# A gated attention and mixture-of-experts block on one core: unwanted products between stages, attention begun with two batches, scaled queries, small first loads

## The chip, the cores and the metric

The program runs on one core of one Trainium2 chip. A core has five engines that run side by side and wait for each other through semaphores: TensorE (PE in the profile, PEld for its loading of stationary operands), VectorE (DVE), ScalarE (ACT), GpSimd (POOL) and SyncE (SP). Transfers between the chip's main memory and the on-chip memories are issued from queues of SP, ACT or POOL and run on 16 DMA engines. TensorE writes its products to PSUM, eight banks of 128 by 512 floats here. TensorE's clock is granted by the chip: the profile gives it as a share of full speed.

The metric is the device time of one execution in microseconds (us); lower is better.

## The reference

Two layers on x of shape (64, 128, 128), all float32. The first is cross-attention to a context of 77 rows per batch; the second a block in which each token picks few of 16 experts for its query, key, value and output projections, with self-attention inside a batch.

```python
def _L0_xattn_ref(batch, latent, Wk, Wq, Wv):
    keys = einsum('bpe,fe->bpf', batch, Wk)
    queries = einsum('ble,fe->blf', latent, Wq)
    values = einsum('bpe,fe->bpf', batch, Wv)
    weights = softmax(einsum('ble,bpe->blp', queries, keys) * scale, axis=-1)
    return einsum('blp,bpe->ble', weights, values)
...
    logits = xn @ sn - sigmoid(gates)
    gated = relu(logits)
    ...
    w = softmax(where(mask > 0, gated, -inf), axis=-1)      # few of 16 experts per token
    def moe_proj(p):
        y = einsum('nc,ech->neh', x, p)
        return einsum('ne,neh->nh', w, y)
    q, k, v = (moe_proj(p).reshape(b, t, -1) for p in (q_proj, k_proj, v_proj))
    scores = einsum('bth,bsh->bts', q, k) / sqrt(h)
    attn = softmax(scores, axis=-1)
    o = einsum('bts,bsh->bth', attn, v).reshape(n, h)
    out = einsum('enh,ehc->nc', einsum('ne,nh->enh', w, o), o_proj)
...
x = x + tanh(g_xattn[0]) * _L0_xattn_ref(ctx_1024, _layernorm(x), Wk, Wq, Wv)
x = x + tanh(g_ffn[0]) * _L0_ffn_ref(_layernorm(x), sim_matrix, gates, q_proj, k_proj, v_proj, o_proj)
```

## The kernel before

There are 8192 tokens, 64 tiles of 128. The kernel goes through five stages, one after the other.

`first_stage` (L193 on) does the cross-attention of all batches, four batches to a group, and picks each token's experts. It writes the new x and the expert weights to main memory as `xrow`, in batch order.

`order` (L678 on) sorts tokens by their pair of experts. It makes `place_i` (where each token goes) and `source` (which token stands at each sorted place). `source` comes from 64 accumulated products into the PSUM tile `pi` (L801); after the last one DVE reads `pi` (L811). A count, `flag`, is then read by all engines, and a branch chooses the sparse program (L1304) that this input takes.

`project` (L971 on) gathers the sorted rows with 64 indirect transfers issued by POOL (L980), makes the list of (tile, expert) items with 24 small products (`list_items`, L859) and then, for each item, a product of 128 by 128 by 384 (L1019) that DVE scales and adds up in `acc` (L1024, L1028). Each finished tile is scattered back to batch order in `qkvrow` by an indirect transfer of POOL (L997). The order of items is written out in `in_turn`.

`attend` (L1050 on) is the self-attention. SP loads q, k and v of a group of batches from `qkvrow` (L1068) once all scatters have landed; the groups have 1, 1, 2, 4, 4, ... batches. Each group is a stream of four steps: transposes of q and k with their copies to on-chip memory (`transposed`, L169 and L175; ACT copies q, DVE copies k); score products (L1087) and softmax (L148 row maximum, L150 its scaling by 1/sqrt(C), L155 exponentials); transposed exponentials; products with v (L1110), scaling by DVE into `o` (L1118) and one indirect scatter by POOL per batch to `orow`, sorted again (L1125). `in_steps` (L181) starts one more group at each step and advances all running ones by a step. Five output tiles `o` can be in flight.

`output` (L1137 on) loads the sorted attention rows four tiles at a time with SP (L1147, `fetch`), after all scatters of `attend`. PE transposes each tile (L1150), ACT copies the result (L1151), and for each item PE multiplies by the expert's output weights (L1176), and DVE adds the scaled product to x (L1180). Finished tiles are scattered by POOL to the result (L1158). Four tiles `og` of four token tiles each can be in flight.

A scheduler sets the order of instructions on each engine from the order of the calls and the data; each engine then runs its instructions strictly in that order. `LATER` is a dependency that only orders two instructions of one engine, `SYNC` one with a semaphore.

Of the kernel before, what the change touches and what calls it, by code (L numbers as in the profile page):

```python
# [10 lines left out]
F32 = mybir.dt.float32  # L11
# [11 lines left out]
def gated_xattn_moe_kernel(  # L23
# [33 lines left out]
    nc = tc.nc  # L57

    B, T, C = x.shape
# [82 lines left out]
    std = const.tile([P, B], F32, tag="std", name="std")  # L142
    flag = const.tile([1, 1], I32, tag="flag", name="flag")

    def softmax(small, psc, ex, n, scale=None, many=G):

        nm = small.tile([P, G], F32, tag="nm", name=f"nm_{n}")[:, :many]
        nc.vector.tensor_reduce(nm, psc, AX.X, ALU.max, negate=True)  # L148
        if scale is None:
            nc.vector.tensor_scalar_mul(nm, nm, SCALE)  # L150
        else:
            nc.vector.tensor_mul(nm, nm, scale)
        sums = small.tile([P, G], F32, tag="sums", name=f"sums_{n}")[:, :many]
        for j in range(many):
            nc.scalar.activation(  # L155
                ex[:, j, :],
                psc[:, j, :],
                AF.Exp,
                bias=nm[:, j : j + 1],
                scale=SCALE if scale is None else scale[:, j : j + 1],  # L160
                accum_out=sums[:, j : j + 1],
            )
        return sums

    def transposed(bank, pool, src, rows, cols, tag, n, copy=None, many=G):

        pt = bank(f"pt_{tag}_{n}")
        for j in range(many):
            nc.tensor.transpose(  # L169
                pt[:cols, j * rows : (j + 1) * rows],  # L170
                src[:, j, :],
                ident[:rows, :rows],
            )
        dst = pool.tile([cols, G * rows], F32, tag=tag, name=f"{tag}_{n}")
        (copy or nc.scalar.copy)(dst[:, : many * rows], pt[:cols, : many * rows])  # L175
        return dst

    def by_batch(rows, b0, n, lo, hi):
        return rows[b0 * T : (b0 + n) * T, lo:hi].rearrange("(b t) c -> t b c", t=T)

    def in_steps(streams, lag=1):  # L181

        running, step = [], 0
        while streams or running:
            if streams and step % lag == 0:
                running.append(streams.pop(0))
            for s in list(running):
                if next(s, "done") == "done":
                    running.remove(s)
            step += 1  # L190
# [487 lines left out]
    def order(ctx, begun, place_i, source, ahead):  # L678
# [106 lines left out]
        for b0 in range(0, B, K):  # L785
            r = slice(b0, b0 + K)
            nc.vector.tensor_tensor(
                at_hi[:, r, :],
                colh[:, None, :].to_broadcast([P, K, NTILE]),
                hi[:, r, None].to_broadcast([P, K, NTILE]),  # L790
                ALU.is_equal,
            )
            nc.vector.tensor_tensor(
                at_lo[:, r, :],
                col[:, None, :].to_broadcast([P, K, P]),
                lo[:, r, None].to_broadcast([P, K, P]),
                ALU.is_equal,
            )
            for b in range(b0, b0 + K):
                nc.scalar.mul(at_id[:, b, :], at_hi[:, b, :], ids[:, b : b + 1])  # L800
                nc.tensor.matmul(  # L801
                    pi[:, b // NB, :],
                    at_lo[:, b, :],
                    at_id[:, b, :],
                    start=(b % NB == 0),
                    stop=(b % NB == NB - 1),
                )

        R = [P, B // NB, NTILE]
        whose, found = t("whose", R), t("found", [P, NTILE])  # L810
        nc.vector.scalar_tensor_tensor(  # L811
# [159 lines left out]
    def project(ctx, source, items, given, xg, acc):  # L971
# [44 lines left out]

        def weighted(name, slot, w, s, there, add):
            py = ps.tile([P, 512], F32, tag="tmp", name=name)
            nc.tensor.matmul(  # L1019
                py[:, : 3 * C], slot, w_flat[:, bass.ds(w, 3 * C)], start=True, stop=True  # L1020
            )
            scale = xg[:, bass.ds(s, 1)]
            if add:
                nc.vector.scalar_tensor_tensor(  # L1024
                    there, py[:, : 3 * C], scale, there, ALU.mult, ALU.add
                )
            else:
                nc.vector.tensor_scalar(there, py[:, : 3 * C], scale, None, ALU.mult)  # L1028
# [11 lines left out]
        def more(i):  # L1040
# [2 lines left out]
            there = acc[:, bass.ds(at_acc.tile_of(i), 3 * C)]  # L1043
            weighted(f"pm_{i}", slot, at_w[2].of(i), at_s[2].tile_of(i), there, True)

        in_turn(ready, fixed, more, store, True, 3)
        return made

    @with_exitstack
    def attend(ctx, place_i, stored, acc):  # L1050

        io = ctx.enter_context(tc.tile_pool(name="io_c", bufs=5))
        work = ctx.enter_context(tc.tile_pool(name="work_c", bufs=3))
# [11 lines left out]
        def load(g):  # L1065
            b0, n = starts[g], sizes[g]
            qkv = acc[:, b0 * 3 * C : (b0 + n) * 3 * C].rearrange("p (b c) -> p b c", b=n)
            behind(nc.sync.dma_start(qkv, by_batch(qkvrow, b0, n, 0, 3 * C)), stored)  # L1068
            return qkv

        loaded = {g: load(g) for g in range(5)}
        made = []

        def group(g):
            b0, n = starts[g], sizes[g]
            qkv = loaded.pop(g)
            if g + 5 < len(sizes):
                loaded[g + 5] = load(g + 5)
            qT = transposed(bank, work, qkv[:, :, 0:C], P, C, "qT", g, many=n)
            kT = transposed(  # L1080
                bank, work, qkv[:, :, C : 2 * C], P, C, "kT", g, copy=nc.vector.tensor_copy, many=n
            )
            yield

            psc = bank(f"psc2_{g}").rearrange("p (b s) -> p b s", s=P)[:, :n, :]
            for j in range(n):
                nc.tensor.matmul(  # L1087
                    psc[:, j, :],
                    qT[:, j * P : (j + 1) * P],
                    kT[:, j * P : (j + 1) * P],  # L1090
                    start=True,
                    stop=True,
                )
            ex = work.tile([P, G, T], F32, tag="ex2", name=f"ex2_{g}")[:, :n, :]
            sums = softmax(small, psc, ex, f"f_{g}", many=n)
            yield

            gsum = small.tile([P, G], F32, tag="gsum2", name=f"gsum2_{g}")[:, :n]  # L1100
            nc.vector.reciprocal(gsum, sums)
            nc.vector.scalar_tensor_tensor(
                gsum, gsum, tg_f, std[:, b0 : b0 + n], ALU.mult, ALU.mult
            )
            exT = transposed(bank, work, ex, P, P, "ex2T", g, many=n)
            yield

            po = bank(f"po_{g}").rearrange("p (b c) -> p b c", c=C)[:, :n, :]
            for j in range(n):
                nc.tensor.matmul(  # L1110
                    po[:, j, :],
                    exT[:, j * P : (j + 1) * P],
                    qkv[:, j, 2 * C : 3 * C],
                    start=True,
                    stop=True,
                )
            o = io.tile([P, G, C], F32, tag="o", name=f"o_{g}")
            nc.vector.tensor_tensor(  # L1118
                o[:, :n, :], po, gsum[:, :, None].to_broadcast([P, n, C]), ALU.mult
            )  # L1120
            for j in range(n):
                b = b0 + j
                apart(
                    made,
                    nc.gpsimd.indirect_dma_start(  # L1125
                        orow,
                        bass.IndirectOffsetOnAxis(ap=place_i[:, b : b + 1], axis=0),
                        o[:, j, :],
                        None,
                    ),  # L1130
                )

        in_steps([group(g) for g in range(len(sizes))])
        return made

    @with_exitstack
    def output(ctx, source, items, xg, scattered, acc):  # L1137

        io = ctx.enter_context(tc.tile_pool(name="io_d", bufs=4))
        slots = ctx.enter_context(tc.tile_pool(name="slots_d", bufs=8))  # L1140
        ps = ctx.enter_context(tc.tile_pool(name="ps_d", bufs=8, space=bass.MemoryType.PSUM))
        oT = acc[:, : NTILE * P]
        rows_out = out.rearrange("b t c -> (b t) c")

        def fetch(t):
            og = io.tile([P, G, C], F32, tag="og", name=f"og_{t}")
            behind(nc.sync.dma_start(og, by_batch(orow, t, G, 0, C)), scattered)  # L1147
            pt = ps.tile([P, 512], F32, tag="tmp", name=f"pto_{t}")
            for j in range(G):
                nc.tensor.transpose(pt[:, j * P : (j + 1) * P], og[:, j, :], ident)  # L1150
            nc.scalar.copy(oT[:, t * P : (t + G) * P], pt)  # L1151

        made = []

# [13 lines left out]
        at_w = [Offsets(nc.tensor, items, 3, first) for first in (0, NTILE, NFIX)]  # L1168
        at_s = [Offsets(nc.vector, items, 4, first, SROW, C, E) for first in (0, NTILE, NFIX)]
        def ready(t):  # L1170
            if t % G == 0:
                fetch(t)

        def weighted(name, slot, w, s, there):
# [129 lines left out]
    with tc.If(most_active < 3) as sparse:  # L1304
        with tc.tile_pool(name="ordered", bufs=1) as ordered:
# [1 line left out]
            _, _, _, limits, facts, _, items_b = begun["pairs"]  # L1307
            given = (ahead, begun["met"], limits, facts, items_b)
            stored = project(source, items, given, xg, acc)
            scattered = attend(place_i, stored, acc)  # L1310
            output(source, items, xg, scattered, acc)
    with sparse.Else():
        dense()
# [42 lines left out]
```

## Time and profile before

| | |
|---|---|
| median of 3 runs | 642.78 us (641.19 to 646.51) |
| the profiled execution | 644.02 us, of which 642.3 are the span from first to last instruction |
| busy: PE / PEld | 457.9 / 337.7 us (71% / 53%) |
| busy: DVE / ACT / POOL | 371.1 / 232.9 / 298.2 us (58% / 36% / 46%) |
| granted clock of PE, mean | 0.846 |
| instructions | 9774 |

The costliest groups stand like this on the page: line, engine, operation, what is written from what, count, busy time, mean of one in ns, then the engine's idle time just before them and what ended most of it.

```profile
L1019 PE MATMUL py<-w_all,xT 128*128 x256 | 106.6, 512 | 31.0 <-issue 23.2
L1024 DVE SCALAR_TENSOR_TENSOR acc<-pm,xg,acc 128x384 f32 x104 | 63.8, 613 | 24.5 <-PE py L1019 12.9
L1125 POOL DMA_INDIRECT orow<-o,place_i x64 | 61.9, 967 | 52.6 <-DVE o L1118 16.8
L1158 POOL DMA_INDIRECT out_dram<-xg,source x64 | 62.0, 968 | 60.7 <-DVE xg L1180 50.3
L1180 DVE SCALAR_TENSOR_TENSOR xg<-pz,xg 128x128 f32<-128x128 f32 x128 | 41.9, 345 | 28.1 <-PE pz L1176 20.3
```

A float32 product is two records of PE (so 64 x 2 items of `pz` are 256 records), a transpose is one. "issue" is idle time for which the profile shows no reason, "remote" and "another core or an unknown queue" one whose releaser it can't name.

### The profile page before, as it was taken

To read this page: it belongs to the slowest core of one execution; us is meant where nothing else is said; L and a number is where in the kernel's file an instruction comes from. 1 tells how busy PE (TensorE), PEld (TensorE's weight loads), DVE (VectorE), ACT (ScalarE), POOL (GpSimd) and SP (SyncE) were. 2 spreads that over 40 slices of the span, in tenths; PEclk is the share of its full clock that TensorE was granted. 3 is DMA by queue.
4 is the path that set the end of the run, shared out by engine and by line. 5 is a ranking of instruction groups with operands and counts; after the bars stand their busy time and mean duration, and the time that the engine had idled before them with its cause. 6 is when DMAs were issued, how large, how long until landed. Compare 5 with 4: busy or idle time off the path is not lost. (4 is left out here: it accounts for less than half of the span.)

```text
span 642.3 us, 9774 instructions
## 1 busy us (share of the span) xinstructions
PE 457.9 (71%) x2467; PEld 337.7 (53%) x2467; DVE 371.1 (58%) x1196; ACT 232.9 (36%) x846; POOL 298.2 (46%) x328
## 2 busy tenths in 40 slices
PE   2999999756723226999999994677665457876771
PEld 1898986432411003555555552567555356765761
DVE  4379999977310014888888884244333225666552
ACT  2689898547000002232223120244433225332300
POOL 4134344400777760333422556165666604555564
PEclk9999999855855566999999998597978659899777
DMA  8954221210222220122211323895111143121111
GB/s 212 248 154 118 73 76 39 74 38 1 61 60 57 57 60 12 62 88 75 87 62 38 123 107 134 295 379 199 45 42 45 42 122 108 62 90 41 39 47 36
DMA packets 53173, 59.56 MB, mean 93 GB/s; under 512 B 6455, under 2 KB 44919, under 8 KB 53111
## 3 DMA queue, kind: packets, MB, share of 16 engines
q1 hardware_dynamic: 40928, 32.41, 16.7%
q0 software_dynamic: 10240, 25.71, 12.4%
q10 hardware_dynamic: 1943, 0.74, 0.6%
q8 instruction: 24, 0.39, 0.3%
q14 instruction: 38, 0.31, 0.2%
HBM read 33.14 MB, written 25.69 MB: 92 GB/s over the span
## 5 line engine op out<-in xcount | busy, mean ns | idle before, releaser
L1019 PE MATMUL py<-w_all,xT 128*128 x256 | 106.6, 512 | 31.0 <-issue 23.2
L997 POOL DMA_INDIRECT qkvrow<-acc,source x64 | 62.1, 970 | 99.4 <-DVE acc L1024 91.5
L1158 POOL DMA_INDIRECT out_dram<-xg,source x64 | 62.0, 968 | 60.7 <-DVE xg L1180 50.3
L1019 PE MATMUL pm<-w_all,slot 128*128 x208 | 86.9, 504 | 0.0
L1125 POOL DMA_INDIRECT orow<-o,place_i x64 | 61.9, 967 | 52.6 <-DVE o L1118 16.8
L980 POOL DMA_INDIRECT xg<-xrow,source x64 | 60.7, 948 | 44.8 <-issue 44.8
L1024 DVE SCALAR_TENSOR_TENSOR acc<-pm,xg,acc 128x384 f32 x104 | 63.8, 613 | 24.5 <-PE py L1019 12.9
L1019 PEld LDWEIGHTS py<-w_all,xT 128*128 128x128 f32 x256 | 45.5, 198 | 60.5 <-issue 32.5
L1028 DVE TENSOR_SCALAR acc<-py,xg 128x384 f32<-128x384 f32 x64 | 39.2, 615 | 53.2 <-remote 24.7
L990 ACT COPY xT<-ptx 128x128 f32<-128x128 f32 x64 | 16.6, 262 | 123.0 <-remote 70.2
L1176 PE MATMUL pz<-w_all,acc 128*128 x256 | 52.6, 313 | 10.2 <-DVE xg L1180 4.9
L1180 DVE SCALAR_TENSOR_TENSOR xg<-pz,xg 128x128 f32<-128x128 f32 x128 | 41.9, 345 | 28.1 <-PE pz L1176 20.3
L1176 PE MATMUL pn<-w_all,slot 128*128 x208 | 46.4, 319 | 15.3 <-ACT acc L1151 5.2
L1019 PEld LDWEIGHTS pm<-w_all,slot 128*128 128x128 f32 x208 | 40.8, 197 | 29.7 <-issue 3.0
L1180 DVE SCALAR_TENSOR_TENSOR xg<-pn,xg 128x128 f32 x104 | 35.9, 345 | 26.0 <-PE pz L1176 9.8
L1042 ACT COPY slot<-xT 128x128 f32 x104 | 28.9, 298 | 57.4 <-PE pm L1019 49.2
L1176 PEld LDWEIGHTS pz<-w_all,acc 128*128 128x128 f32 x256 | 41.9, 217 | 14.8 <-DVE xg L1180 7.4
L1024 DVE SCALAR_TENSOR_TENSOR acc<-py,xg,acc 128x384 f32<-128x384 f32 x64 | 38.5, 612 | 18.1 <-remote 11.4
L1176 PEld LDWEIGHTS pn<-w_all,slot 128*128 128x128 f32 x208 | 35.3, 218 | 20.3 <-issue 7.0
L169 PE MATMUL pt_ex2T<-ident,ex 128*128 128x128 f32 x64 | 20.8, 349 | 25.9 <-ACT ex L155 15.1
L989 PE MATMUL ptx<-ident,xg 128*128 128x128 f32 x64 | 18.3, 291 | 26.4 <-issue 26.4
L989 PEld LDWEIGHTS ptx<-ident,xg 128*128 128x128 f32 x64 | 9.1, 144 | 41.2 <-issue 32.9
(212 smaller groups left out, 939.9 us busy)
## 6 DMA issues: line engine op xcount, KB each, us to landing
acc<-qkvrow SPq DMA_DIRECT2D x15, 768.0 KB
xt<-in_x_dram SPq DMA_DIRECT2D x16, 256.0 KB
og<-orow SPq DMA_DIRECT2D x16, 256.0 KB
xrow<-xr SPq DMA_DIRECT2D x7, 576.0 KB
ct<-in_ctx_dram SPq DMA_DIRECT2D x16, 154.0 KB
xg<-xrow,source POOLq DMA_INDIRECT x64
qkvrow<-acc,source POOLq DMA_INDIRECT x64
orow<-o,place_i POOLq DMA_INDIRECT x64
```

The costliest lines, as they stand in the source:

```text
L169: nc.tensor.transpose(pt[:cols, j * rows : (j + 1) * rows], src[:, j, :], ident[:rows, :rows],)
L980: nc.gpsimd.indirect_dma_start(xg[:, t * SROW : t * SROW + ROW], None, xrow, bass.IndirectOffsetOnAxis(ap=source[:, t : t + 1], axis=0),)
L989: nc.tensor.transpose(pt[:, :P], xg[:, t * SROW : t * SROW + C], ident)
L997: nc.gpsimd.indirect_dma_start(qkvrow, bass.IndirectOffsetOnAxis(ap=source[:, t : t + 1], axis=0), acc[:, t * 3 * C : (t + 1) * 3 * C], No ...
L1019: nc.tensor.matmul(py[:, : 3 * C], slot, w_flat[:, bass.ds(w, 3 * C)], start=True, stop=True)
L1024: nc.vector.scalar_tensor_tensor(there, py[:, : 3 * C], scale, there, ALU.mult, ALU.add)
L1028: nc.vector.tensor_scalar(there, py[:, : 3 * C], scale, None, ALU.mult)
L1042: nc.scalar.copy(slot, xT[:, bass.ds(at_x.tile_of(i), P)])
L1125: nc.gpsimd.indirect_dma_start(orow, bass.IndirectOffsetOnAxis(ap=place_i[:, b : b + 1], axis=0), o[:, j, :], None,),
L1158: nc.gpsimd.indirect_dma_start(rows_out, bass.IndirectOffsetOnAxis(ap=source[:, t : t + 1], axis=0), xg[:, t * SROW : t * SROW + C], None,),
L1176: nc.tensor.matmul(py[:, :C], slot, w_flat[:, 3 * C :][:, bass.ds(w, C)], start=True, stop=True)
L1180: nc.vector.scalar_tensor_tensor(there, py[:, :C], scale, there, ALU.mult, ALU.add)
```

## The change

- A helper `between` makes a number of products of the identity with itself into a PSUM bank that nobody reads, each held behind the one before on PE. It is called three times: 8 products after the last product of `order`; 42 after the last product of `project`, and attention's first transpose is held behind them; 18 in `output`, the first of which waits for the fourth-last scatter of `attend`, and the first transpose of `output` is held behind them.
- `in_steps` starts two streams at its first step (before, one), and one per step after that. The load of attention's second group is issued from ACT's queue.
- Attention's query copy multiplies by 1/sqrt(C) (an activation in place of a copy); its softmax no longer scales the row maximum, and its exponentials have the scale 1.
- `output` loads 1, 1 and 2 tiles first and then four at a time, the second load from ACT's queue; six `og` tiles can be in flight.

In the built programs, PE's order in attention begins with the transposes of both first groups, then both score products, and from there on the groups come one step earlier. In `project` the order of all engines is unchanged.

```diff
-    def softmax(small, psc, ex, n, scale=None, many=G):
+    def softmax(small, psc, ex, n, scale=None, many=G, scaled=False):
...
-        if scale is None:
+        if scale is None and not scaled:
             nc.vector.tensor_scalar_mul(nm, nm, SCALE)
-        else:
+        elif scale is not None:
             nc.vector.tensor_mul(nm, nm, scale)
...
-                scale=SCALE if scale is None else scale[:, j : j + 1],
+                scale=scale[:, j : j + 1] if scale is not None else 1.0 if scaled else SCALE,
...
+    def between(bank, n, old, kind):
+
+        unused = bank("unused")
+        for k in range(n):
+            new = nc.tensor.matmul(unused[:, :P], ident, ident, start=True, stop=True)
+            if k == 0:
+                tc.add_manual_dep(new.ins, old.ins.name, kind, reason="between stages")
+            else:
+                tc.add_manual_dep(new.ins, done.ins.name, LATER, reason="between stages")
+            done = new
+        return done
...
-    def in_steps(streams, lag=1):
+    def in_steps(streams, at_once=1):
...
-            if streams and step % lag == 0:
-                running.append(streams.pop(0))
+            for _ in range(at_once if step == 0 else 1):
+                if streams:
+                    running.append(streams.pop(0))
...
+        between(lambda _: bank("po"), 8, last, LATER)
         R = [P, B // NB, NTILE]
...
-            behind(nc.sync.dma_start(qkv, by_batch(qkvrow, b0, n, 0, 3 * C)), stored)
+            queue = nc.scalar if g == 1 else nc.sync
+            behind(queue.dma_start(qkv, by_batch(qkvrow, b0, n, 0, 3 * C)), stored)
...
+        idle = between(bank, 42, last_product, LATER)
...
-            qT = transposed(bank, work, qkv[:, :, 0:C], P, C, "qT", g, many=n)
+            scale = lambda to, at: nc.scalar.mul(to, at, SCALE)
+            qT = transposed(
+                bank, work, qkv[:, :, 0:C], P, C, "qT", g, copy=scale, many=n,
+                later=idle if g == 0 else None,
+            )
...
-            sums = softmax(small, psc, ex, f"f_{g}", many=n)
+            sums = softmax(small, psc, ex, f"f_{g}", many=n, scaled=True)
...
-        in_steps([group(g) for g in range(len(sizes))])
+        in_steps([group(g) for g in range(len(sizes))], 2)
...
-        io = ctx.enter_context(tc.tile_pool(name="io_d", bufs=4))
+        io = ctx.enter_context(tc.tile_pool(name="io_d", bufs=6))
...
+        sizes = {0: 1, 1: 1, 2: 2}
+        sizes.update({t: G for t in range(G, NTILE, G)})
...
+        idle = between(bank, 18, scattered[-4], SYNC)
+
         def fetch(t):
-            og = io.tile([P, G, C], F32, tag="og", name=f"og_{t}")
-            behind(nc.sync.dma_start(og, by_batch(orow, t, G, 0, C)), scattered)
...
+            n = sizes[t]
+            og = io.tile([P, G, C], F32, tag="og", name=f"og_{t}")[:, :n, :]
+            queue = nc.scalar if t == 1 else nc.sync
+            behind(queue.dma_start(og, by_batch(orow, t, n, 0, C)), scattered)
+            pt = bank(f"pto_{t}")
+            for j in range(n):
+                new = nc.tensor.transpose(pt[:, j * P : (j + 1) * P], og[:, j, :], ident)
+                if t == 0:
+                    tc.add_manual_dep(new.ins, idle.ins.name, LATER, reason="between stages")
+            nc.scalar.copy(oT[:, t * P : (t + n) * P], pt[:, : n * P])
...
-            if t % G == 0:
+            if t in sizes:
                 fetch(t)
```

## The prediction

> **What bounds the kernel now.** I read the page's slices first, for the granted clock of TensorE (PE) beside its load.
>
> ```profile
> PE   2999999756723226999999994677665457876771
> PEclk9999999855855566999999998597978659899777
> ```
>
> A slice is 16 us. No engine is full over the span, and the clock falls to half at three places: slices 9 to 16, 26, and 32 to 33. They hold or touch the joints between stages: the ordering stage into the projections (156 us), projections into attention (393 us), attention into the output (510 us). I then asked for busy time and clock in stretches cut at these joints (start:end, length, busy us and records of PE, PEld, DVE, ACT, POOL, clock, DMA share, GB/s).
>
> ```profile
> 156.40:161.10 4.70, 0.04 (x1) 0.00 (x0) 3.51 (x13) 0.00 (x0) 1.51 (x2) 0.50 0.00 0
> 161.10:165.10 4.00, 3.93 (x19) 2.51 (x20) 1.95 (x7) 0.00 (x0) 3.09 (x4) 0.50 0.33 74
> 392.80:405.30 12.50, 0.00 (x0) 0.00 (x0) 2.06 (x4) 0.00 (x0) 5.97 (x7) 0.68 0.42 144
> 405.30:414.40 9.10, 7.49 (x30) 6.19 (x30) 3.49 (x14) 2.84 (x10) 0.97 (x1) 0.50 0.98 337
> 414.40:430.90 16.50, 14.43 (x106) 12.10 (x106) 7.83 (x23) 9.04 (x35) 8.71 (x9) 1.00 1.06 378
> 509.70:519.60 9.90, 0.00 (x0) 0.02 (x1) 0.38 (x1) 0.00 (x0) 3.87 (x4) 0.50 0.29 85
> 519.60:530.20 10.60, 9.24 (x39) 8.54 (x40) 3.86 (x11) 3.55 (x11) 0.00 (x0) 0.50 0.44 125
> 530.20:545.00 14.80, 11.52 (x84) 9.82 (x83) 8.82 (x31) 7.40 (x25) 7.74 (x8) 0.99 0.35 108
> ```
>
> Each joint is an idle PE, then a start at half clock: 4.0, 9.1 and 10.6 us, 23.7 us in all, with PE nearly always busy. The chain of waits says what these starts hang on (start, us, what).
>
> ```profile
> 402.77 2.45 DMA acc<-qkvrow
> 405.36 0.45 PE pt_qT L169
> 406.55 0.77 PE psc L1087 x2
> ...
> 516.56 2.91 DMA og<-orow
> 519.61 1.10 PE pto L1150 x4
> 520.85 0.59 ACT acc L1151
> 521.49 1.72 PE pz L1176 x6
> ...
> 587.16 8.66 another core or an unknown queue
> ```
>
> A load of rows just scattered lands, and PE's work follows one by one. The last line is another thing: pauses which nothing in the profile releases, with all engines but POOL standing still, mostly after six or so indirect transfers back to back. They hold the rest of both stages. The timeline of one of them in attention:
>
> ```profile
> 448.27 0.69 DVE L148 TENSOR_REDUCE nm_f<-psc 128x4 f32<-128x512 f32 x1 [0.85 <-PE psc L1087]
> 451.65 0.69 DVE L175 COPY kT<-pt_kT 128x512 f32<-128x512 f32 x1 [2.69 <-remote]
> 452.26 0.16 DVE L150 TENSOR_SCALAR nm_f<-nm_f 128x4 f32<-128x4 f32 x1
> 452.51 0.37 ACT L155 ACTIVATE ex<-psc,nm_f 128x128 f32<-128x128 f32 x1 [2.35 <-DVE kT L175]
> ```
>
> The small scaling at 452.26 stands behind a copy that came late, and the exponential waits for it.
>
> **Price of an unwanted product.** Attention's score products are of the same form (float32, 128 by 128 by 128, two records each). Two took 0.87 us at half clock (411.3 us) and four 0.89 us at full (415.9 us): 0.43 and 0.22 us each.
>
> **Eight products after the ordering stage.** At half clock 8 x 0.43 = 3.4 us: from PE's last product (156.4) to 159.9. Behind them in PE's queue are the reading of the flag, the branch, and the 24 records of the item list, which start at 161.1, when DVE has made the first mask. DVE's own way over flag and branch took 0.8 us (158.2 to 159.0); so PE is there at 160.7, with 0.4 us to spare. If PE's branch met a pause such as attention shows (2.2 us), the list would come 1.8 us late: the far end. On the other side, the list took 4.7 us at half clock; at full it would be held by DVE's eight masks (0.3 us each, and a handover) at about 3.0 us: 1.7 us less at best. From 172 to 249 us products come singly, several us apart, so a head start buys one or two more products before that, of 0.62 us each on DVE, which paces the stage from 249 on. I take -0.8 us, between +1.8 and -1.7.
>
> **Forty-two products before attention.** PE stops at 392.8; the first of them waits for DVE to have read its bank, at the latest 394.9. Then 42 x 0.22 = 9.3 us: they end between 402.1 and 404.2, before the first load lands (405.3). In the old run the clock fell at 397.3, 4.5 us after PE stopped; now PE is idle for 3.2 us at most. Were the clock to fall first, some eight products would cost 0.43 and the end move to 405.8: 0.5 us late.
>
> **Two batches side by side, the second load on ACT's queue.** ACT is idle there, so nothing but its own first copy is behind the waiting load. Both loads, and the 384 KB third behind the first on SP's queue, share the DMA (share 0.98 in that stretch), so I let the second land up to 0.7 us after the first. PE's new order is four transposes, both score products, then batch group 2, then the transposed exponentials of 0 and 1. By hand, with full-clock durations: second transposes to 406.2, scores 406.5 and 406.75, row maxima 407.5, ACT's query copy of group 2 first (its 384 KB at 380 GB/s land near 407), exponentials 407.9 to 408.9, scores of group 2 near 409.1 (before 411.1), of group 3 near 412 (before 415.75), of group 4 near 415.6 (before 419.56). The stage is 4.0 us ahead there. If full clock holds only for the first few us, half of it; if loads are not late, 5.5 us. I take -4.0, between -2.0 and -5.5.
>
> **Queries scaled.** It removes 18 scalings of nm_f (0.16 us each, 2.9 us of DVE) and makes 18 query copies of ACT into scaled ones. The only scaled copy from PSUM of 128x128 took 0.367 us (L262) against 0.27 for a plain one: +0.1 us at most on 0.58, ACT having room (36% busy). What counts is the place: the exponential needs only the row maximum now. Its waits behind DVE's nm_f, kT and o are 6.9 + 4.0 + 3.2 = 14.1 us. That is the upper bound, 0 the lower less 1.8 us for slower copies. Most of it isn't gained: in a pause the output tile o follows the same late kT copy in DVE's order, and POOL waits for o. The next round gains. I take -2.0, between +1.8 and -14.
>
> **Output.** The first 256 KB load (2.91 us) becomes 64 KB on SP's queue, 64 KB on ACT's and 128 KB. PE's order has the transposes of all three ahead of the first product, and together they are as many bytes, so the third lands about when the old one did, near 519.5. But the old chain of four transposes (1.1), a 512-wide copy (0.6) and the first product at 521.49 becomes two full-clock transposes and a copy already made: first product near 519.8, -1.7 us. From there to 530.2 PE ran 13 products (13 x 0.43 = 5.6) and three sets of four transposes (3 x 0.87 = 2.6). At full clock these are 4.2 us; DVE's 13 accumulations at 0.35 to 0.39 (5.0) then come last: 3.5 us less at most. The 18 products wait for the fourth-last scatter: issued 510.36, landed 2.2 us later, 512.6. Wholly at half clock they last 7.7 us, to 520.4: 0.8 us past the load, and the price of their presence. If the clock rises after the 4 to 5 us that it took at 161, they end at 518.7 and cost nothing. -1.7 - 3.5 + 0.5 = -4.7 at best; pauses follow from 540 on, so I take -3.5, between 0 and -5.2. The two more buffers of og hold as many tiles (16) in flight as before.
>
> **Two rules weighed.** Row: 23.7 us at half clock with PE busy, half of which, 11.8 us, could go. The Trainium skill, "TensorE: Matmul & The Clock Gate", section "Part 1: The HAM clock gate (the "warmup" mystery)", says that the ramp penalty is under 1% of a typical kernel span, which here is an estimate of 6.4 us: clock alone would then give not even that, and with the reordering the sum would be nearer -7. Second row: from 505.2 to 506.7 PE made four transposes and the clock still fell to half. The same page, section "Part 4: PE-mode transpose", says that transposes don't count as work in the same way; attention's first work is transposes, and by this rule the clock falls again soon after the unwanted products, the -4.0 becomes -2.5.
>
> **Sum.** -0.8 - 4.0 - 2.0 - 3.5 = -10.3 us. The profiled execution took 644.02 us (span 642.3 and 1.7 around it), so 633.7; the median of the runs is 1.24 us below the profiled one: 632.5 us.
>
> **Rivals.** (1) The head start is given back. Attention's 64 scatters need 64 x 1.27 = 81.5 us of POOL and took 103; what is over are the gaps beside the pauses. If a pause is bound to what POOL has written, or comes sooner when POOL runs without gaps, the stage ends as before and only the output's start is left, perhaps 1 to 4 us: 639 to 642. For it: pauses follow runs of back-to-back transfers. Against: they come at the same place in the work, which moves too. (2) The scaling was what made pauses long, and most of the 14.1 us comes back: 632.5 - 10 = 622. For it: the timeline above. Against: o's place. (3) Slower: denser scatters bring more pauses. Place: the output, where one held the chain for 8.66 us. Two more of these cost 17.3 us against the 10.3 gained: 649.8. It decides from the second one on; one more alone gives 641. Nothing shows that a pause is added, only that they follow dense runs. (4) The change doesn't do what it says: clock stays at half at the joints. The reordering and scaling then stay, -5: 637.8; against it, the projections held full clock on such products.
>
> **Chances.** Forecast, 626 to 637: 0.52. Rivals 1 and 4, 637 to 645: 0.30. Rival 2, below 626: 0.10. Rival 3, above 649: 0.08. The range 623 to 644 leaves out rival 3, the far part of rival 2 and a little of 1. A measurement tells about 1% from no change, 636.4 and 649.2: faster 0.60 (rival 2 and nearly all of the forecast), same 0.32, slower 0.08.
>
> **What would show it.** Clock 1.0 in the stretches from the item list, the first query transpose and the first output transpose on, in place of 0.50; the products' records ending before each load lands (after it, the overrun is right); the scores of group 4 about 10 us after the first transpose in place of 14.2; exponentials directly behind the row maximum; the first output scatter about 10 us after the first load in place of 14.7. It would be wrong if the last attention scatter came as long after the first load as before (111.4 us), or if the output's scatters, 105.6 us from first to last, took longer.

## The result, and the profile after

The changed kernel takes 644.06 us (median of 20 runs, 639.73 to 648.96), the kernel before on the same chip 644.53 us (20 runs). The ratio is 1.0004, 95% interval 0.9987 to 1.0022: no change. The forecast was 632.5 us, 623 to 644.

The page's slices after the change, TensorE's load and granted clock:

```profile
PE   2999999758731235999999998877787488776771
PEclk9999999855855555999999999997787589789887
```

The half clock of slices 26 and 33 is gone; slice 32, the end of attention, still stands at 5 (6 before). The stretches at the joints, cut at the same events as before the change (start:end, length, busy us and records of PE, PEld, DVE, ACT, POOL, clock, DMA share, GB/s):

```profile
161.90:166.40 4.50, 4.43 (x25) 2.81 (x25) 1.93 (x7) 0.00 (x0) 3.46 (x4) 0.61 0.30 69
408.00:417.10 9.10, 7.04 (x52) 5.84 (x52) 4.67 (x17) 4.26 (x17) 1.31 (x2) 1.00 1.04 362
417.10:433.60 16.50, 11.86 (x89) 9.97 (x87) 6.54 (x15) 8.72 (x37) 10.34 (x11) 0.94 1.06 382
511.40:518.10 6.70, 6.65 (x36) 6.68 (x37) 0.00 (x0) 0.00 (x0) 1.94 (x2) 0.58 0.31 89
518.10:528.70 10.60, 8.59 (x66) 7.41 (x65) 5.31 (x16) 6.69 (x24) 1.49 (x2) 1.00 0.84 225
```

Attention's and the output's starts have a clock of 1.00 where they had 0.50, and PE gets 52 records done in 9.1 us instead of 30, and 66 in 10.6 instead of 39. At the item list the clock hardly rose in this profile (0.61). The chain of waits at the same places:

```profile
405.96 4.53 DMA acc<-qkvrow
410.53 0.45 PE pt_qT L169 x2
...
509.05 2.27 DMA orow<-o,place_i
511.45 6.90 PE unused L184 x36
518.81 0.71 PE pz L1214 x4
```

The first product of the output comes at 518.81 us instead of 521.49, and attention's chain now begins at the third load instead of the first (405.36 is the first load's product in the chain before, 410.53 the third load's now). Cut at POOL's transfers, the two profiled executions compare like this (differences of starts in the timeline of POOL; `T` is PE's first query transpose):

| stretch | before | after |
|---|---|---|
| last qkvrow scatter to last orow scatter | 114.5 us | 110.5 us |
| of it, T to first orow scatter | 6.6 | 7.4 |
| last orow scatter to first out_dram scatter | 17.1 | 13.3 |
| first to last out_dram scatter | 105.6 | 110.0 |

So both head starts are there, 4.0 and 3.8 us, and the last row, in which the diff edits nothing past the first loads, takes 4.4 us of them. Most of what is left goes into the time up to the last qkvrow scatter, 2.8 us longer in this one profile; over all profiles that time varies by 5 us (last paragraph of the experiments).

### The profile page after: what moved, and what is told of

Same layout as the page of the kernel before. It is cut to its first block, busy times and chain, and to the rows that moved or that the text cites. A ratio compares the mean times of both kernels' runs of the same rounds, so it can differ in the third digit from the quotient of the medians.

```text
span 641.6 us, 9986 instructions
## 1 busy us (share of the span) xinstructions
PE 477.7 (74%) x2603; PEld 356.6 (56%) x2603; DVE 369.2 (58%) x1178; ACT 232.7 (36%) x848; POOL 299.0 (47%) x328
## 5 line engine op out<-in xcount | busy, mean ns | idle before, releaser
L1014 POOL DMA_INDIRECT qkvrow<-acc,source x64 | 62.3, 973 | 101.0 <-DVE acc L1041 92.3
L1214 PE MATMUL pz<-w_all,acc 128*128 x256 | 53.4, 317 | 8.8 <-DVE xg L1218 6.3
L1214 PE MATMUL pn<-w_all,slot 128*128 x208 | 44.9, 309 | 17.8 <-DVE xg L1218 8.3
L1041 DVE SCALAR_TENSOR_TENSOR acc<-py,xg,acc 128x384 f32<-128x384 f32 x64 | 38.5, 611 | 21.7 <-remote 17.1
L1214 PEld LDWEIGHTS pn<-w_all,slot 128*128 128x128 f32 x208 | 34.2, 212 | 22.5 <-issue 11.5
L1228 ACT COPY slot<-acc 128x128 f32 x104 | 24.7, 295 | 22.4 <-PE pz L1214 11.7
```

Of the source, the lines that this page charges most:

```text
L1014: nc.gpsimd.indirect_dma_start(qkvrow, bass.IndirectOffsetOnAxis(ap=source[:, t : t + 1], axis=0), acc[:, t * 3 * C : (t + 1) * 3 * C], No ...
L1041: nc.vector.scalar_tensor_tensor(there, py[:, : 3 * C], scale, there, ALU.mult, ALU.add)
L1214: nc.tensor.matmul(py[:, :C], slot, w_flat[:, 3 * C :][:, bass.ds(w, C)], start=True, stop=True)
```

## The experiments

All ratios are against the kernel before, run beside them on the same chip. The runs of one letter shared a chip and each letter had another, so a comparison between letters is one of two such ratios. At first I had three theories: **R**, what a stage gains at its start reaches the end; **E**, the prediction's first rival, that pauses and POOL give a head start back; **O**, that the parts are worth something but with opposite signs.

**The parts, and starts held back.** `e1` has the output as before, `e2` has only the output's part; `e3` and `e4` hold a start back with 40 more unwanted products:

```diff
-        idle = between(bank, 18, scattered[-4], SYNC)
+        idle = between(bank, 58, scattered[-4], SYNC)
```
```diff
-        idle = between(bank, 42, last_product, LATER)
+        idle = between(bank, 82, last_product, LATER)
```

> The changed kernel with the output as it was before: the 8 and the 42 unwanted products, two batches side by side and the scaled queries stay. Theory R (rigid: what a stage gains at its start reaches the end) by the terms of the prediction: -0.8 - 4.0 - 2.0 = -6.8 us against before, some 637 to 638 us. Theory E (elastic: what follows a start is paced by something that does not move with it, so a head start is given back within the stage or in the next): within 1.5 us of before, with the first attention scores 3 to 5 us sooner after the first transpose and the last output scatter not sooner. Theory O (the parts are worth what they cost, but with opposite signs: attention gains the 4.9 us of the one profile, the output's new loads lose them): about 4 to 5 us faster than before.

> The kernel before with the output's part of the change alone: 18 unwanted products, loads of 1, 1, 2 and then 4 tiles, six buffers. Theory R: -3.5 us against before, 641 us. Theory E: within 1.5 us of before, the first output scatter some 4 us sooner after the first load and the rest of the stage longer by as much (about 110 us from first to last scatter, as in the changed kernel, where it was 105.6 before). Theory O: slower than before, by up to 4 us.

> The changed kernel with 58 unwanted products ahead of the output in place of 18: 40 more at 0.22 us each hold the first transpose back by about 8 us, with all loads landed and the clock high. Theory R: about 8 us slower than the changed kernel, 652 us. Theory E: less than 3 us slower, 644 to 647, and the scatters closer together (100 to 104 us from first to last in place of 110). Theory O says nothing of its own here and goes with R.

> The changed kernel with 82 unwanted products ahead of attention in place of 42: 40 more hold the first query transpose back by about 8 us, to 416 us. Theory R: 8 us slower than the changed kernel less some 2 us that were waits for the third and fourth load, so about 650 us. Theory E: less than 3 us slower, the last attention scatter at most 3 us later than in the changed kernel, the scatters closer together.

Measured: `e1` 647.93 us, ratio 1.0069 (1.0041 to 1.0097): 0.7% slower. `e2` 641.19 us, 0.9955 (0.9933 to 0.9977): the output's part gives 2.9 us, near its term of 3.5. `e3` 1.0086 (1.0064 to 1.0109), `e4` 1.0057 (1.0036 to 1.0078): 5 and 3 us slower than the changed kernel for starts some 9 us later, between R and E. So the loss lies in the edits ahead of the output, yet in `e1`, apart from the time up to the last qkvrow scatter, the stretch that is longer than before (109.5 us from first to last out_dram scatter, against 105.6) is the output, whose code there is that of before. Theory O had the signs the wrong way round.

**Single parts beside the output's part.** Each of the next four is `e2` with one edit more: the 8 products, the 42, two batches side by side with the load on ACT's queue, the scaled queries.

> The kernel with the output's part alone (0.9955 of before, 641.2 us) and beside it only the 8 unwanted products ahead of the item list. The four parts ahead of the output cost 3 to 4 us together, where the prediction had -6.8. By the prediction's term this one is -0.8 us (between +1.8 and -1.7). Rival, that it is the one that costs: +3 us or more, with the time from the last gather to the first qkv scatter 17.7 us in place of 16.4, as three of four profiles with the products show it (the fourth had 16.4).

> The output's part alone and beside it only the 42 unwanted products ahead of attention. Prediction's part: full clock at the first transposes saves some 2 us of the 4 us, so -1 to -2 us against the output's part alone. Rival, that it costs: the products end after the first load or leave the clock lower later in attention (0.75 to 0.81 from 420 to 515 us with all four parts, 0.83 without), +2 us or more.

> The output's part alone and beside it only two batches side by side, the second load on ACT's queue. Prediction's part: some -2 us of the 4 (at half clock). Rival, that it costs: the first output rows come later (both small batches wait for the third load, and the first scatter comes 13 to 15 us after the last qkv scatter in place of 12.3), and as the scatters run nearly without a break what POOL begins later ends later: +1 to +3 us.

> The output's part alone and beside it only the scaled queries. Prediction: -2.0 us (between +1.8 and -14). Rival, that it costs: ACT's query copy is longer or the order of DVE's instructions around the row maximum is worse for the pauses, +1.8 us or more.

These ran on another chip, on which the kernel before took 543.43 us, as the pauses were missing there (last section). Ratios: 0.9926, 0.9951, 0.9924 and 0.9969, each with 0.2 to 0.3% to either side. `e2` itself was not run there, so they can only be held against each other: `f4` is 2.3 us above `f1` and 2.4 above `f3` (2.0 and 2.1 either way), the rest is too close together. The profiles split them in another way: from first to last out_dram scatter 90.8 and 90.9 us in `f1` and `f2`, 92.3 and 92.9 in `f3` and `f4`.

**The changed kernel less one part.** `g1` is the changed kernel again; `g2` begins the batches one by one; `g3` scales behind the row maximum again; `g4` has neither the 8 nor the 42 products.

> The changed kernel itself, for what is compared with it here. Where the kernel before takes about 644 us: 1.000 of it again. Where it takes about 543 us, as in the runs of the single parts (there the other engines hardly ever stand still while POOL issues transfers): theory G (the pauses gave the head starts back) expects that there all of it is seen, -8 us or 0.985; theory F (POOL's first scatter of attention counts, and two batches side by side make it later) expects about the output's part and a little more, -4 to -5 us or 0.992.

> The changed kernel with the batches begun one by one as before (the ACT queue's load, the 42 products and the scaled queries stay). Theory F: the first scatter 1.5 to 2.5 us sooner after the first transpose (some 5.8 us in place of 7.4 to 9.0), and the time 2 us or more below the changed kernel's where the chip has pauses, about the same where it has none (there the stage with the two side by side took 82.0 us from first to last scatter, POOL's own pace, and 85.8 one by one). The prediction's term: 2 us slower than the changed kernel.

> The changed kernel with the scaling back behind the row maximum. The prediction's term: 2 us slower than the changed kernel. Rival, that the scaled queries are what costs ahead of the output: 2 us or more faster.

> The changed kernel without the 8 and the 42 products (the 18 stay). The prediction's terms: 2.8 us slower than the changed kernel (0.8 and half of 4.0). Rival, that the products are what costs (loads issued later behind them: in the run with the 42 alone the first load was issued 4.25 us after the last qkv scatter, in the others 2.7 to 3.5): 1 to 3 us faster.

Measured, on a chip with pauses: 1.0006 (0.9984 to 1.0029), 0.9990 (0.9970 to 1.0010), 0.9940 (0.9922 to 0.9959), 0.9999 (0.9979 to 1.0019). Undoing the scaled queries gains 4 us (`g3` against `g1`), and the stretch that becomes shorter is again the output's scatters: 104.9 us in place of 111.4. A scaling in attention does no work there. I therefore laid the built programs' instruction orders side by side, in the output's items, which no edit touches. PE's products stand in the same order in all kernels. DVE's accumulations do not; this is a part of both queues of the changed kernel (`pn` are items' products, `pz` a tile's first and second):

```
PE's products       pn_12 pz_3_0 pn_13 pz_2_1 pn_14 pz_4_0 pn_15 pz_3_1 pn_16 pz_5_0
DVE, before         pn_12 pz_3_0 pn_13 pz_2_1 pn_14 pz_4_0 pn_15 pz_3_1 pn_16 pz_5_0
DVE, changed        pz_2_1 pn_12 pz_3_0 pn_13 pz_3_1 pn_14 pz_4_0 pn_15 pz_4_1 pn_16
```

Before, 226 of 232 accumulations stand in the place of their product. In the changed kernel 53 of those from the 18th to the 131st stand ahead of it (48 by one product, four by three, one by six) and 66 one behind: DVE waits for a product still to be made, while a finished one waits for DVE. The register loads for the items' offsets move along. The scheduler that orders the instructions did this, and small edits elsewhere flip it: `e1`, `f3`, `f4`, `g1`, `g2`, `g4` have the changed order, `e2`, `e3`, `e4`, `f1`, `f2`, `g3` that of before. That is just the split of the output's times: on the chips with pauses 109.0 to 111.4 us from first to last out_dram scatter with the changed order, 104.6 to 107.2 with that of before. `e3` and `e4` flipped back, so that starts held back by 9 us cost them only 5 and 3.

**The order alone.** A correlation, and most of those kernels also have scaled queries; so two runs with only the order changed. `h1` pins it in the changed kernel; `h2` is `e2` with the changed order forced on DVE, by such a dependency along the list of names.

```diff
-            nc.vector.scalar_tensor_tensor(there, py[:, :C], scale, there, ALU.mult, ALU.add)
+            new = nc.vector.scalar_tensor_tensor(there, py[:, :C], scale, there, ALU.mult, ALU.add)
+            if in_order:
+                tc.add_manual_dep(new.ins, in_order[-1].ins.name, LATER, reason="as made")
+            in_order.append(new)
```

`h3` and `h4` add to `h1` one edit in attention, against the late first scatter. `h3` has

```diff
-            for _ in range(at_once if step == 0 else 1):
+            for _ in range(at_once if step == 0 else at_once < 2 or step > 1):
```

and `h4` begins the batches one by one (`in_steps` without the 2).

> The changed kernel with one thing pinned: DVE takes the output's accumulations in the order in which PE makes the products. Theory D (the order of DVE's queue in the output is what took the gain): the output's scatters take 104 to 106 us from first to last in place of 110 to 111, and the time is 4 to 5 us below the changed kernel's, 0.993 of before (where the chip has no pauses: some 2 us below). Theory Q (the scaled queries cost by themselves, in attention or through ACT): as the changed kernel, 1.000 of before, 109 to 111 us.

> The output's part alone (0.9955 of before), queries not scaled, all orders as in that kernel but for DVE's accumulations in the output, which stand in the order that the changed kernel has. Theory D: 109 to 111 us from first to last scatter of the output and 4 to 5 us slower, 1.002 to 1.004 of before (where the chip has no pauses: some 2 us slower than 0.993). Theory Q: unchanged, 0.9955 and 104 to 106 us.

> The changed kernel with the order pinned, and the third group of batches begun one step later, so that the first two do not stand behind its load. Theory F (POOL's first scatter of attention counts): the first scatter 5 to 6 us after the first transpose in place of 7.4 to 9.0, the scatters from first to last no longer than 98 us, and 1 to 2 us faster than the changed kernel with the order pinned. If POOL waits for the groups after the first two instead, no faster.

> The changed kernel with the order pinned and the batches begun one by one as before. Theory F: first scatter 5.8 us after the first transpose, but 100 us from first to last as in the one-by-one runs: within 1 us of the changed kernel with the order pinned. The prediction's term for two side by side: 2 us slower than it.

Measured: `h1` 639.13 us, 0.9914 (0.9887 to 0.9941), output scatters in 104.0 us; `h2` 645.89 us, 1.0016 (0.9998 to 1.0034), in 109.2 us. The views of these scatters (duration, then first and last start), in the order changed kernel, `h1`, `e2`, `h2`:

```profile
L1196 POOL DMA_INDIRECT out_dram<-xg,source x64: 964/971/982, 526.1 to 636.1; - x64
L1196 POOL DMA_INDIRECT out_dram<-xg,source x64: 967/972/982, 527.4 to 631.4; - x64
L1192 POOL DMA_INDIRECT out_dram<-xg,source x64: 967/972/977, 527.8 to 632.3; - x64
L1219 POOL DMA_INDIRECT out_dram<-xg,source x64: 967/972/977, 533.3 to 642.5; - x64
```

In both pairs the built programs differ in DVE's queue in the output alone; the other engines' queues are the same, instruction for instruction. The order alone, put in or taken out, moves the time by 3.9 us (1.8 either way; `h2` against `e2`) and by 5.8 us (2.1 either way; `h1` against the changed kernel). Such differences are of two ratios, times 644 us, their half-widths added as squares. Theory D stands, Q falls. Where it is lost can be seen in DVE's own records: from the start of its 17th to that of its 132nd accumulation it needs 52.7 to 54.7 us in the six profiles with the changed order on chips with pauses, 46.4 to 50.5 in the ten others; from there to the last one it is 47.7 to 53.4 us and 47.8 to 53.7, no difference. One place, from the 57th accumulation on, in the timeline of DVE of the changed kernel (start, duration, and in brackets the idle time ahead and its releaser):

```profile
544.18 0.34 DVE L1218 SCALAR_TENSOR_TENSOR xg<-pn,xg 128x128 f32 x1
546.80 0.35 DVE L1218 SCALAR_TENSOR_TENSOR xg<-pz,xg 128x128 f32<-128x128 f32 x1 [2.28 <-PE pz L1214]
548.31 0.35 DVE L1218 SCALAR_TENSOR_TENSOR xg<-pn,xg 128x128 f32 x1 [1.16 <-issue]
```

and the same place of the stage in `h1`:

```profile
545.74 0.34 DVE L1218 SCALAR_TENSOR_TENSOR xg<-pz,xg 128x128 f32<-128x128 f32 x1
547.12 0.35 DVE L1218 SCALAR_TENSOR_TENSOR xg<-pn,xg 128x128 f32 x1 [1.04 <-issue]
547.50 0.35 DVE L1218 SCALAR_TENSOR_TENSOR xg<-pz,xg 128x128 f32<-128x128 f32 x1
548.93 0.35 DVE L1218 SCALAR_TENSOR_TENSOR xg<-pn,xg 128x128 f32 x1 [1.08 <-PE pz L1214]
```

3.4 us of standing here against 2.1, at one of several such places up to the 132nd accumulation. Whether the wait out of turn or the register loads that moved with it cost the more was not separated.

`h3` 638.34 us, 0.9905 (0.9882 to 0.9927); `h4` 636.87 us, 0.9883 (0.9859 to 0.9907): both below `h1`, `h3` by 0.6 us and `h4` by 2.0 (2.3 either way for both), which is not clear of noise; `g2` against `g1` says 1.0 us (1.9 either way) the same way. `h4` is 1.2% below the kernel before. Attention's first scatter is the reason to look there. In the timeline of the changed kernel the exponentials of the first two batches stand on ACT behind the third group's query copy, which waits for its load:

```profile
408.07 0.33 PE L169 MATMUL pt_qT<-ident,acc 128*128 128x128 f32 x1 [0.76 <-DMA acc<-qkvrow]
410.53 0.44 PE L169 MATMUL pt_qT<-ident,acc 128*128 128x128 f32 x2 [0.81 <-DMA acc<-qkvrow]
411.01 0.38 ACT L1100 ACTIVATE qT<-pt_qT 128x256 f32<-128x256 f32 x1 [2.07 <-PE pt_qT L169]
411.29 0.36 ACT L155 ACTIVATE ex<-psc,nm_f 128x128 f32<-128x128 f32 x1
415.48 0.97 POOL L1150 DMA_INDIRECT orow<-o,place_i  x1 [12.10 <-ACT ex L155]
```

and in `h3`, where that group comes a step later:

```profile
405.74 0.33 PE L169 MATMUL pt_qT<-ident,acc 128*128 128x128 f32 x1 [0.72 <-DMA acc<-qkvrow]
407.53 0.37 ACT L155 ACTIVATE ex<-psc,nm_f 128x128 f32<-128x128 f32 x1 [0.93 <-DVE nm_f L148]
410.89 0.97 POOL L1150 DMA_INDIRECT orow<-o,place_i  x1 [9.81 <-issue]
```

From first transpose to first scatter it is 7.4 to 9.0 us in eight profiles with two batches side by side, 6.3 in the ninth (`e4`, where all loads had landed), 5.2 in `h3`, and 4.7 to 6.6 one by one. The scatters that follow are closer together side by side (96.5 to 99.1 us from first to last; `h3` 99.9, one by one 99.8 to 102.9; chip with pauses), so from the last qkvrow scatter to the last orow scatter `h1` has 111.7 us and `h4` 111.6: in the stage itself side by side gains nothing. But the first scatter, 15.2 us after the last qkvrow scatter in `h1` and 11.5 in `h4`, does not decide either: theory F is not shown.

**The other terms,** measured on `h4`, where the output's order no longer moves: `j1` without the 8 and the 42 products, `j2` with the scaling behind the row maximum.

> The kernel with the order pinned and the batches one by one (0.9883 of before), without the 8 and the 42 products. The prediction's terms (0.8 and about half of 4.0): 2.8 us slower, 0.9925. Rival, that POOL's transfers and the pauses set the pace and the products gain only at the first scatter (11.45 us after the last qkv scatter in place of 12.3): under 1 us slower, 0.9883 to 0.99.

> The same kernel with the scaling back behind the row maximum. The prediction's term: 2.0 us slower, 0.9915. Rival 2 of the prediction (the scaling made the pauses long): 8 us or more slower. Rival, that the order of DVE's queue in the output was all that the scaled queries changed: the same time, 0.988.

`j1` 0.9921 (0.9890 to 0.9952), `j2` 0.9943 (0.9922 to 0.9964). The products are worth 2.4 us by this pair (2.5 either way) and -0.5 by `g4` against `g1` (1.9 either way), with two batches side by side: neither is clear of zero. The scaled queries are worth 3.9 us (2.1 either way). In attention orders still move with these edits: in `j1` and `j2` PE makes all scores of group 4 behind the transposed exponentials of group 3, in `h4` in turn with them, and in `j2` later groups differ too. So each figure is that of the edit with the order that came with it.

**The eight products in all profiles.** The item list stands like this on PE in the changed kernel and in `h4`:

```profile
161.97 4.45 PE L876 MATMUL pf<-is_nth,items_b 128*5 128x256 bf16 x24 [1.17 <-DVE is_nth L872]
163.24 2.78 PE L876 MATMUL pf<-is_nth,items_b 128*5 128x256 bf16 x24 [1.28 <-DVE is_nth L872]
```

On chips with pauses there are eleven profiles with the eight products. In seven (`e1`, `e3`, `e4`, `g2`, `g3`, `h4`, `j2`) the list took 2.78 us, in the other four 4.45 to 4.88; in the five without the products it took 4.69 to 5.28. At the stage's end this is not seen: the last qkvrow scatter starts at 401.5 to 403.6 us in those seven and at 399.6 to 404.8 in the five.

## Why the prediction was wrong

- **The step that failed: what the change moves.** The sum priced the output at -3.5 us as if its queues were those of before. They were not: DVE's order in it had changed, and that could be read from the built programs beforehand; of the orders, the section on the change names PE's in attention and those in `project`, none in the output. The missing term is +3.9 to +5.8 us. Without it the changed kernel takes 639.1 us (`h1`), inside the range though above the 632.5. The prediction's own sign of being wrong was there: the output's scatters took 110.0 us from first to last, longer than 105.6.
- **Two batches side by side,** with the clock, -4.0 us: the milestone chosen, scores of group 4 about 10 us after the first transpose, came true (417.74, 9.7 us), but not by this means. It is 11.5 us in `g1`, the same kernel, 10.8 in `h1` and 9.8 in `h4`, where the batches begin one by one; so the part gained here is not the second batch's. The first two batches' exponentials came 3.2 us after the first transpose (`h4`: 1.8), behind the third group's query copy, whose load PE got 2.5 us after that transpose, where "near 407" meant 1.6. POOL, which has 81.5 us of transfers to issue in this stage, then started 0.8 us later after the transpose than before. From the last qkvrow to the last orow scatter the stage takes 110.5 to 112.3 us in the five profiles with attention as changed, 112.1 to 115.2 in the three with attention as before (chips with pauses): a gain of some 2 us for the 6.0 of this term and the scaled queries'. Side by side costs 2.0 us against one by one (2.3 either way): the sign of the term was wrong, or it is nothing.
- **42 products:** they ended ahead of the load here (407.31, first transpose 408.07) and the clock was 1.00. In `e1`, `e3`, `g2`, `h1`, `h4` and `j2` their beginning was at half clock, they lasted 11.3 instead of 9.6 us, and the first transpose came 6.4 to 6.8 us after the last qkvrow scatter in place of 5.6 to 5.9. The first load was issued later there too, by 0.4 to 1.1 us, and in `f2`, with the products done in 9.6 us, both were late as well (6.6 us); so what of this the products cost is not separated. With the 8 they give the 2.4 us of `j1`'s pair (2.5 either way), for 0.8 and about half of 4.0.
- **Eight products,** -0.8 us: they were out of the way before the list (160.8 and 161.97), as priced. The faster list, priced at about 3.0 us, came in seven of eleven profiles (2.78), not in the one of the changed kernel (4.45, against 4.74). That it reaches the end of the stage is not shown.
- **Queries scaled,** -2.0 us: right in sign, and the pair says 3.9 (2.1 either way), with the orders that moved in attention. The exponentials' waits behind DVE went from 14.1 us to 0.7 here (6.2 in `g1`), so most of them were not on the path, as the prediction held. Rival 2 (the scaling made the pauses long) would have been 8 or more; the longest pause of ACT is 4.85 us before and 4.48 after.
- **Output,** -3.5 us: right. `e2` measures 2.9 (1.4 either way); the first scatter came 10.9 us after the first load was issued, for "about 10".
- **Rival 1** came nearest to the time, 639 to 642 us, by luck, for a wrong reason. With the order of before in the output, starts are not given back: `e3` is 11.1 us above `h1` (2.3 either way) for a first output transpose that is 8.8 us later after the last scatter, and `e4` 9.2 us above it (2.2 either way) for an end of attention that is 8.2 later.
- **Rivals 3 and 4:** the lost time is in one section of one queue and goes away with the order, so it is not two more pauses; and the clock did rise at two of the three joints.
- **The two rules.** The Trainium skill, "TensorE: Matmul & The Clock Gate", section "Part 1: The HAM clock gate (the "warmup" mystery)", holds the ramp penalty to under 1% of a typical span; the 2.4 us of `j1` (2.5 either way) are 0.4% and lie below that. Its section "Part 4: PE-mode transpose" says that transposes don't count as work in the same way; the drop in clock that I made of it did not come: 1.00 up to 417.1 us and 0.94 to 433.6, with transposes among the products. A longer stretch of transposes alone was not tried.

## What to carry to other kernels

When a scheduler orders the instructions, compare the order of every queue in the parts that the diff does not touch, and hold it against the order of its producer; one engine taking its work out of turn cost 4 to 6 us here, where the edits kept in `h4`, with the order pinned, bring 7.5. Pin an order that matters. And judge an edit in a stage by the stage's end, not by a step on the way: a first scatter 3.7 us sooner (`h4` against `h1`) did not move attention's last one.

## What the runs showed of the hardware

The kernel before took about 100 us less on one chip: 543.43 us, in the runs beside `f1` to `f4`, against 643.65 to 644.87 beside the result and the other letters. From first to last, POOL's 64 gathers took 78.9 us in the profiles of `before` and `f1`. In the first all other engines stand for most of the time while they are issued (`before`, a stretch of the windows view):

```profile
176.00:186.00 10.00, 3.51 (x6) 1.47 (x6) 1.48 (x3) 0.27 (x1) 7.56 (x9) 0.64 0.25 59
```

and in the second, on the other chip, they do not (`f1`, the same stretch; the code of this stage is the same):

```profile
176.00:186.00 10.00, 10.00 (x37) 5.82 (x36) 8.92 (x16) 3.42 (x15) 7.55 (x8) 1.00 0.24 60
```

PE is busy for 10.00 of 10 us in place of 3.51 with the same load on POOL and the DMA. So the pauses are no property of the program alone. What makes them on some chips was not tried and stays open, as does why the scheduler turned the order with some edits and not with others.
